# A fused adaLN transformer block: new places for transposes, reciprocals and statistics, and a small product moved to GpSimd

## The chip, the cores and the metric

The kernel runs on one core of a Trainium2 chip. A core has a matrix engine (TensorE, PE in the profile), a vector engine (VectorE, DVE), an activation engine (ScalarE, ACT), a general engine (GpSimd, POOL) and a queue engine (SyncE, SP) that here only issues DMAs. Each engine executes its own instructions in order and waits for others by semaphores. The metric is the time of one execution in microseconds on the device; lower is better. All arithmetic is in 32-bit floats.

## The reference

For 16 sequences (batches) of 1024 tokens with 256 features, an attention layer and a mixture-of-experts layer are computed, both behind a modulated layer norm:

```
mod = silu(c) @ wmod                              # shift, scale, gate, per batch, twice
h   = layernorm(x) * (1 + ca) + sa
xn  = layernorm(h) * gamma + beta
q, k = rope(xn Wq + bq), rope(xn Wk + bk);  v = xn Wv + bv     # 16 heads of 16
p   = softmax(causal(q k^T / 4));  o = (p v) Wo + bo
x   = x + ga * (h + o)
h2  = layernorm(x) * (1 + cb) + sb
x   = x + gb * scatter_add(experts(h2[top_idx]))  # 8 experts, 512 rows each, gelu
```

Two layer norms stand in front of attention, one on x and one on h. Each needs, per row, a mean, a variance, the power r = (variance + eps)^-0.5, and the product n = -mean * r; then the row is scaled by r and shifted by n.

## The kernel before

**The loop.** After a start (modulation, constants, batch 0's own preparation) the kernel runs one long loop: batch b, group G of four heads (0 to 3), step n (0 to 9). I write (G, n) for a place in it. A step treats one block of keys against the queries of one half of the sequence (c = 0: queries 0 to 511, c = 1: 512 to 1023); steps 1 and 5 treat two small blocks at once and are called two-block steps. In every step TensorE makes, for four heads, the scores `s` of this group (L682) and, one group ahead, the products `m` (L605) whose row maxima the next group will need. They come in two runs (bursts): scores of heads 0 and 1 with maxima products of heads 2 and 3, then the other way round. ScalarE takes the exponential of each `s` (L695), GpSimd zeroes what lies above the diagonal (L700), VectorE takes the maximum of each `m` (L623 and L627; the latter is a masked form with a separate accumulator read). `s` and `m` share six PSUM tiles.

**Between the runs and behind them.** TensorE does one item between the runs (`first`) and one behind the second (`second`). One is the product of the last step's probabilities with the values (`product(last)`, L729); the other is a piece for the next batches: the transposes `ptx` of the normalised rows (L485, evicted by ScalarE, L486), projections to queries and keys (L510, with two vector products each for the rotary angles, L517), to values (L541), or the output projection (L821). If there is no piece, the values are split into two halves. The transposes (`turns`) are placed in two-block steps: (0,1), (0,5), (1,1), (3,5). All these pieces share one other PSUM tile, `misc`.

**Normalising two batches ahead.** `steps_h` makes the norms. Its parts have names: `x0` to `x3` and `h0` to `h3` are statistics of a 256-wide row tile (VectorE, L387), `moments` merges them (L392), `power` makes r by two small GpSimd instructions (L397, L398), `less` makes n by one small vector instruction (L406), `norm` applies both (ScalarE, L415), and larger GpSimd passes scale, shift, add a bias, gate and add onto x. The table `H_AT` gives each part its place (G, n) for either half of the sequence. Parts of VectorE go into the list `inside`: they are taken one at a time behind each of the step's four maxima, and what is left is taken behind the last (`drain`). Parts of the other engines go into `extra`, which is emitted at the end of the step.

**The sums' inverse.** The values carry a column of ones, so each half's output ends with the softmax sums. When a half is done (c = 0 at step 3, c = 1 at step 0 of the next group), `finish` copies the output (ScalarE, L744), sends the sums to DRAM and back as `den` (two DMAs on SP, L784 and L785), and returns what is left: `inverse` (the reciprocal on VectorE, L789, a row to DRAM, L791, four broadcasts back as `rec`, L794), `scaled` (GpSimd, L797) and, in odd groups, `joined` (GpSimd, L800). `to_do` places them: the inverse into `inside` two steps after the half is done, the GpSimd parts at the end of the fifth step after it (c = 0) or the fourth (c = 1).

The orders on PE, VectorE, ScalarE and GpSimd are as written; SP's order comes from the scheduler and follows the program closely. After the loop come the experts, which the change does not touch.

Of the kernel before, what the change touches and what calls it, by code (L numbers as in the profile page):

```python
# [11 lines left out]
F32 = mybir.dt.float32  # L12
# [4 lines left out]
ALU = mybir.AluOpType  # L17
AX = mybir.AxisListType

P = 128  # L20
# [7 lines left out]
def adaln_block_kernel(  # L28
# [27 lines left out]
    nc = tc.nc  # L56
# [5 lines left out]
    NT = L // P  # L62
    GH = 4
# [5 lines left out]
    TC = QC // P  # L69
# [7 lines left out]
    eps = const.tile([P, NT], F32, name="eps")  # L77
    nc.vector.memset(eps, EPS)
    mhalf = const.tile([P, NT], F32, name="mhalf")
    nc.vector.memset(mhalf, -0.5)  # L80

    C, E = top_idx.shape
# [113 lines left out]
    with ExitStack() as actx:  # L196
# [178 lines left out]
        def steps_h(b, half, named=False):  # L375

            s = S[b]
            mine = {}  # L380
            passes = nc.vector if (b, half) == (0, 0) else nc.gpsimd

            def stat(of, i):
                if i == 0:
                    mine["st"] = wk.tile([P, TC, 6], F32, name=f"st_{of}_{b}_{half}", tag="st")
                src = s["x"][:, half * TC + i, :] if of == "x" else s["h", half][:, i, :]
                nc.vector.bn_stats(mine["st"][:, i, :], src)  # L387

            def moments(of):
                mine["mv"] = wk.tile([P, TC, 2], F32, name=f"mv_{of}_{b}_{half}", tag="mv")  # L390
                for i in range(TC):
                    nc.vector.bn_aggr(mine["mv"][:, i, :], mine["st"][:, i, :])  # L392
                mine["mean"] = mine["mv"][:, :, 0]

            def power(of):
                mine["r"] = wk.tile([P, TC], F32, name=f"rstd_{of}_{b}_{half}", tag="rstd")
                nc.gpsimd.tensor_tensor(mine["r"], mine["mv"][:, :, 1], eps[:, :TC], ALU.add)  # L397
                nc.gpsimd.tensor_tensor(mine["r"], mine["r"], mhalf[:, :TC], ALU.pow)  # L398

            def whole(of):  # L400
                moments(of)
                power(of)

            def less_mean(of):
                mine["n"] = wk.tile([P, TC], F32, name=f"nmr_{of}_{b}_{half}", tag="nmr")
                nc.vector.scalar_tensor_tensor(mine["n"], mine["mean"], -1.0, mine["r"], ALU.mult, ALU.mult)  # L406

            def norm(of, u):
                if of == "x" and u == 0:
                    s["h", half] = lk.tile([P, TC, D], F32, name=f"h_{b}_{half}", tag="h")  # L410
                if u == 0 and not named:
                    less_mean(of)
                h = s["h", half]
                for i in (2 * u, 2 * u + 1):
                    nc.scalar.activation(  # L415
                        h[:, i, :],
                        s["x"][:, half * TC + i, :] if of == "x" else h[:, i, :],
                        AF.Identity,
                        bias=mine["n"][:, i : i + 1],
                        scale=mine["r"][:, i : i + 1],  # L420
                    )

            def row(n):
                return (bo_bc[:, None, :] if n is None else s["mod"][:, n : n + 1, :]).to_broadcast([P, 2, D])

            def turn(u, n, op):
                h = s["h", half][:, ts(u, 2), :]
                passes.tensor_tensor(h, h, row(n), op)  # L428

            def rest(u, n, op):  # L430
                if n is None and u == 0 and b > 0:
                    mine["rest"] = lk.tile([P, TC, D], F32, name=f"r_{b}_{half}", tag="r", bufs=1)
                elif n is None and u == 0:
                    if half == 0:
                        s["rest"] = big_tile([P, NT, D], "r_0")
                    mine["rest"] = s["rest"][:, ts(half, TC), :]
                r = mine["rest"][:, ts(u, 2), :]
                (passes if n is None else nc.gpsimd).tensor_tensor(r, s["h", half][:, ts(u, 2), :] if n is None else r, row(n), op)

            def onto(u):  # L440
                xh = s["x"][:, half * TC + 2 * u : half * TC + 2 * u + 2, :]
                nc.gpsimd.tensor_tensor(xh, xh, mine["rest"][:, ts(u, 2), :], ALU.add)

            if named:
                pieces = {f"{of}{i}": lambda of=of, i=i: stat(of, i) for of in "xh" for i in range(TC)}
                for of in "xh":
                    pieces[of + " moments"] = lambda of=of: moments(of)
                    pieces[of + " power"] = lambda of=of: power(of)
                    pieces[of + " less"] = lambda of=of: less_mean(of)
                for u in range(2):  # L450
                    pieces[f"x norm{u}"] = lambda u=u: norm("x", u)
                    pieces[f"scale{u}"] = lambda u=u: turn(u, 1, ALU.mult)
                    pieces[f"shift{u}"] = lambda u=u: turn(u, 0, ALU.add)
                    pieces[f"bias{u}"] = lambda u=u: rest(u, None, ALU.add)
                    pieces[f"h norm{u}"] = lambda u=u: norm("h", u)
                    pieces[f"gate{u}"] = lambda u=u: rest(u, 2, ALU.mult)
                    pieces[f"onto{u}"] = lambda u=u: onto(u)
                return pieces

            return (  # L460
                [("v", lambda i=i: stat("x", i)) for i in range(TC)]
                + [("g", lambda: whole("x"))]
                + [("v", lambda u=u: norm("x", u)) for u in range(2)]
                + [("g", lambda u=u: turn(u, 1, ALU.mult)) for u in range(2)]
                + [("g", lambda u=u: turn(u, 0, ALU.add)) for u in range(2)]
                + [("v", lambda i=i: stat("h", i)) for i in range(TC)]
                + [("g", lambda: whole("h"))]
                + [("g", lambda u=u: rest(u, None, ALU.add)) for u in range(2)]
                + [("v", lambda u=u: norm("h", u)) for u in range(2)]
                + [("g", lambda u=u: rest(u, 2, ALU.mult)) for u in range(2)]  # L470
                + [("g", lambda u=u: onto(u)) for u in range(2)]
            )
# [410 lines left out]
        def steps(places):  # L883
# [7 lines left out]
        OUT = steps([(0, 9), (0, 9), (), ()]), steps([(), (), (0, 2, 8, 9), ()])  # L891

        H_AT = (
            "x0 0 3, x1 0 4, x2 0 6, x3 0 8, x moments 0 9, x power 1 0, x less 1 3, x norm0 1 3, x norm1 1 4, "
            "scale0 1 4, shift0 1 4, scale1 1 6, shift1 1 7, h0 1 8, h1 1 9, h2 2 0, h3 2 2, h moments 2 3, h power 2 3, "
            "bias0 2 4, h less 2 4, bias1 2 6, gate0 2 6, gate1 2 6, h norm0 2 7, onto0 2 7, h norm1 2 8, onto1 3 3",
            "x0 1 4, x1 1 6, x2 2 4, x3 2 6, x moments 2 8, x power 2 9, x less 3 2, x norm0 3 2, x norm1 3 4, "
            "scale0 3 3, shift0 3 4, scale1 3 6, shift1 3 6, h0 3 6, bias0 3 6, h1 3 7, h2 3 8, h3 3 8, bias1 3 8, "
            "gate0 3 9, h moments 3 9, h power 3 9, h less 4 3, h norm0 4 3, gate1 4 3, onto0 4 3, h norm1 4 4, onto1 4 3",
        )  # L900

        def place_h(b, half, at0):
            parts = steps_h(b, half, named=True)
            for entry in H_AT[half].split(", "):
                name, G, n = entry.rsplit(" ", 2)
                dve = name[:2] in ("x0", "x1", "x2", "x3", "h0", "h1", "h2", "h3") or name.endswith(("moments", "less"))
                (inside if dve else extra)[at0 + int(G) * NS + int(n)].append(parts.pop(name))
            assert not parts, parts.keys()

# [13 lines left out]
        with tc.manual_schedule(engines=ORDERED | {ET.SP}):  # L923
# [52 lines left out]
            units, place = maxima(0, 0)  # L976
# [78 lines left out]
        for e in range(E):  # L1055
            for t in range(NCT):
                extra[(B - 2) * NG * NS + e * NCT + t].append(
                    lambda e=e, t=t: gather(cw[:, e, t, :], combine[:, :], widx[:, t, e : e + 1])
                )
        def to_do(finish, c, step):  # L1060

            first, *others = finish(c)
            if step >= ((B - 1) * NG + NG - 1) * NS + mid:
                for n, item in enumerate([first, *others]):
                    extra[step + 1 + n].append(item)
                return
            inside[step + 2].append(first)
            extra[step + (4 if c else 5)].extend(others)

        behind = None  # L1070
        for b in range(B):
            for G in range(NG):
# [3 lines left out]
                for n, parts in enumerate(blocks):  # L1076
# [25 lines left out]
                    product = values if n else behind and behind[0]  # L1102
                    if not product:
                        first, second = [], mine
                    elif mine and units and len(last) == 2:
                        first, second = mine, [lambda: product(last)]
                    elif units and len(mine) == 2:
                        first, second = [lambda: product(last), mine[1]], mine[:1]
# [263 lines left out]
```

## Time and profile before

| what | us |
|---|---|
| median of three runs | 2889.95 |
| the runs | 2884.34, 2889.95, 2890.49 |
| the profiled execution | 2886.74 |
| its span, first to last instruction | 2885.0 |
| PE busy | 2810.8 |
| VectorE busy | 2125.2 |
| ScalarE busy | 1651.1 |
| GpSimd busy | 1562.6 |

The attention loop fills the span from about 95 to 2605 us, about 164 us a batch; the experts follow. TensorE is counted as busy nearly all of the loop, with a mean granted clock of 0.986 of full speed over the span. Its matmuls are pipelined and their ends are modelled, so a matmul that starts late because a PSUM tile isn't free can leave no idle time in the count: the starts in the timeline tell more. In the timeline a row is: start, duration, engine, line, operation, output and inputs, shapes, count; a bracket gives the idle time before it and what ended it.

### The profile page before, as it was taken

Reading aid. Unit: us, or ns where it says so; the run is one execution under the profiler, and the core shown is the slowest. Engines: PE = TensorE matmul, PEld = TensorE weight load, DVE = VectorE, ACT = ScalarE, POOL = GpSimd, SP = SyncE. Lnnn points to the kernel's source line nnn. Section 1 sums busy time; section 2 is a strip of 40 time slices with the busy share of each in tenths; the row PEclk is TensorE's granted clock in tenths of the full one; section 3 lists DMA queues with packets and bytes.
Section 4 is the critical chain, followed back from the end, with each engine's and each line's share of the span. In section 5 each row is a group of like instructions: output and inputs, shape, how many; then the busy total and the mean of one; then the engine's idle time right before and its main releaser. Section 6 shows DMA issues by size and latency. Waiting matters only on the chain.

```text
span 2885.0 us, 62886 instructions
## 1 busy us (share of the span) xinstructions
PE 2810.8 (97%) x22373; PEld 1289.4 (45%) x22373; DVE 2125.2 (74%) x6810; ACT 1651.1 (57%) x3342; POOL 1562.6 (54%) x2063
## 2 busy tenths in 40 slices
PE   5899999999999999999999999999999999997998
PEld 3444444444444444444444444444444444443665
DVE  5777878777787878787877878787878777763554
ACT  2356666666666566666666666656666655653111
POOL 5455464546555555546454655555464666354553
PEclk7899999999999999999999999999999999998999
DMA  4211121222222222212222222222121212134552
GB/s 122 58 44 35 50 71 52 64 56 68 59 56 56 64 61 63 60 51 66 63 59 62 64 54 58 60 67 62 50 71 51 75 41 65 32 95 153 176 184 67
DMA packets 200154, 199.58 MB, mean 69 GB/s; under 512 B 93344, under 2 KB 154208, under 8 KB 199840
## 3 DMA queue, kind: packets, MB, share of 16 engines
q1 hardware_dynamic: 172240, 147.69, 18.9%
q0 software_dynamic: 8448, 24.78, 2.7%
q10 hardware_dynamic: 19152, 23.08, 2.6%
q8 instruction: 177, 2.90, 0.4%
q14 instruction: 137, 1.12, 0.1%
HBM read 118.67 MB, written 75.66 MB: 67 GB/s over the span
## 4 chain that ended last, share of the span: by engine, by line
PE 90%; DMA 3%; DVE 2%; POOL 2%; issue 1%; ACT 1%; SPq 0%; POOLq 0%; DVEq 0%; ACTq 0%
PE s L682 39%; PE o L729 20%; PE pqk L510 9%; PE m L605 7%; PE pw L821 4%; PE pv L541 4%; PE fo L1229 2%; PE ph L1204 2%; PE ptx L485 1%; DMA out_dram<-fy,idx 1%; DMA cur<-out_dram,idx 1%; POOL modg L98 1%; ACT p L695 0%; DMA ops<-rot 0%; DVE nmr_h L406 0%
## 5 line engine op out<-in xcount | busy, mean ns | idle before, releaser
L695 ACT ACTIVATE p<-s 128x512 f32<-128x512 f32 (+1 forms) x2560 | 1278.9, 552 | 895.5 <-PE m L605 797.4
L605 PE MATMUL m<-ko,qo 32*128 32x512 f32 (+3 forms) x6144 | 1439.5, 527 | 7.0 <-DVE mt L623 4.7
L682 PE MATMUL s<-qo,ko 32*128 32x512 f32 (+3 forms) x6144 | 1359.1, 526 | 0.6 <-DMA qo<-max 0.5
L700 POOL TENSOR_SCALAR_AFFINE_SELECT p<-p 128x256 f32<-128x256 f32 x1024 | 416.1, 414 | 1002.4 <-ACT p L695 1001.2
L623 DVE TENSOR_REDUCE mt<-m 128x1 f32<-128x512 f32 x1024 | 673.0, 683 | 203.9 <-PE m L605 184.2
L682 PEld LDWEIGHTS s<-qo,ko 32*128 32x128 f32 x6144 | 514.8, 183 | 597.3 <-issue 423.6
L729 PE MATMUL o<-p,v_pad 128*32 128x512 f32 (+3 forms) x6840 | 652.7, 464 | 3.2 <-POOL p L700 2.8
L627 DVE CUSTOM_DVE_ANT_0 masked<-m,dmask,mt 128x256 f32<-128x256 f32 (+3 forms) x1024 | 511.4, 539 | 142.6 <-PE m L605 132.1
L627 DVE CUSTOM_DVE_ANT_0 masked<-m,dmask 128x512 f32<-128x512 f32 (+3 forms) x1024 | 453.9, 485 | 189.3 <-PE m L605 170.2
L605 PEld LDWEIGHTS m<-ko,qo 32*128 32x128 f32 x6144 | 576.6, 184 | 30.2 <-DVE mt L627 11.2
L729 PEld LDWEIGHTS o<-p,v_pad 128*32 128x32 f32 x6840 | 149.0, 108 | 427.8 <-issue 180.0
L510 PE MATMUL pqk<-xnT,wqk 128*128 128x256 f32 x1024 | 287.3, 405 | 1.8 <-ACT xnT L486 1.3
L510 PEld LDWEIGHTS pqk<-xnT,wqk 128*128 128x128 f32 x1024 | 175.3, 190 | 193.0 <-issue 148.5
L428 POOL TENSOR_TENSOR h<-h,mod 128x512 f32<-128x512 f32 x124 | 157.6, 1274 | 76.5 <-ACT h L415 70.9
L627 DVE DVE_READ_ACCUMULATOR2_ANT mt<- 128x1 f32 x2048 | 168.7, 82 | 0.0
L541 PE MATMUL pv<-wv_sb,xnT 128*128 128x256 f32 x512 | 146.9, 410 | 1.1 <-ACT xnT L486 0.9
L821 PE MATMUL pw<-wo,onT 128*128 128x256 f32 x512 | 144.2, 405 | 0.6 <-DVE onT L778 0.6
L1207 ACT ACTIVATE gT<-ph,b_sb 128x512 f32<-128x512 f32 x64 | 44.0, 687 | 174.1 <-PE ph L1204 169.1
L541 PEld LDWEIGHTS pv<-wv_sb,xnT 128*128 128x128 f32 x512 | 87.9, 191 | 98.5 <-issue 76.5
L517 DVE SCALAR_TENSOR_TENSOR rot<-pqk,bcol,cosT 128x256 f32<-128x256 f32 x256 | 122.0, 477 | 11.6 <-PE pqk L510 8.3
L821 PEld LDWEIGHTS pw<-wo,onT 128*128 128x128 f32 x512 | 86.9, 189 | 89.3 <-issue 70.9
L517 DVE SCALAR_TENSOR_TENSOR rot<-pqk,bcol,sinT 128x256 f32<-128x256 f32 x256 | 121.3, 474 | 0.6 <-DMA ops<-rot 0.6
(122 smaller groups left out, 2239.5 us busy)
## 6 DMA issues: line engine op xcount, KB each, us to landing
ops<-rot SPq DMA_DIRECT2D x128, 256.0 KB
rec<-rec_d SPq DMA_DIRECT2D x504, 32.0 KB
rows<-y SPq DMA_DIRECT2D x62, 256.0 KB
out_dram<-y SPq DMA_DIRECT2D x62, 256.0 KB
w<-in_W_dram SPq DMA_DIRECT2D x14, 1024.0 KB
qo<-ops SPq DMA_DIRECT2D x192, 64.0 KB
ko<-ops SPq DMA_DIRECT2D x192, 64.0 KB
x<-in_x_dram ACTq DMA_DIRECT2D x24, 512.0 KB
```

Source lines behind the costliest of these rows:

```text
L428: passes.tensor_tensor(h, h, row(n), op)
L510: nc.tensor.matmul(ps, lhsT=wqk[:, k, n, e, :], rhs=xt[:, k, ts(u, QW)], start=(k == 0), stop=(k == KC - 1))
L517: nc.vector.scalar_tensor_tensor(s["rot", half, n, e, f][:, ts(u, QW)], ps, bcol[:, n, e : e + 1], tab[:, half * QC + u * QW : half * QC + ...
L541: nc.tensor.matmul(pv, lhsT=S[b]["xnT", t // TC][:, k, ts(t % TC, P)], rhs=wv_sb[:, k, :], start=(k == 0), stop=(k == KC - 1),)
L605: nc.tensor.matmul(sc[:, sum(w[:n]) : sum(w[: n + 1])], lhsT=q[rows, ts(i, P)], rhs=k[rows, c * QC : c * QC + w[n]], start=True, stop=True,)
L623: nc.vector.tensor_reduce(dst, sc[:, 0:w], AX.X, ALU.max, negate=True)
L627: nc.vector.tensor_tensor_reduce(out=masked[:, 0:w], in0=sc[:, 0:w], in1=dmask[:, QC - w : QC], scale=-1.0, scalar=mt[half][:, 0, h, i % T ...
L682: nc.tensor.matmul(sc[:, o:e], lhsT=k[rows, ts(j_, P)], rhs=q[rows, c_ * QC + q0 : (c_ + 1) * QC], start=True, stop=True,)
L695: nc.scalar.activation(p[:, h, 0:end], sc[:, 0:end], AF.Exp, scale=scale)
L700: nc.gpsimd.affine_select(out=mine, in_=mine, compare_op=ALU.is_ge, fill=0.0, base=0, pattern=[[0, 3 - n], [0, n], [1, P]], channel_multip ...
L729: nc.tensor.matmul(acc[c][W * g : W * (g + 1), q0:q1], lhsT=v[:, j, h * VW + 1 - DH * (G % 2) : h * VW + 1 - DH * (G % 2) + W], rhs=p[:, g ...
L821: nc.tensor.matmul(po, lhsT=s["onT", c][:, k, ts(t, P)], rhs=s["wo"][:, k, :], start=(k == 0), stop=(k == KC - 1),)
```

## The change

It has four parts. (1) In a two-block step that has a piece (a turn), the piece goes between the two runs and the values behind the second; before, the values went between and the piece behind. (2) `power` now also makes n, by two GpSimd multiplications (mean times r, times a constant tile of -1), and the vector instruction `less` is gone, with its places in `H_AT`. (3) The inverse of c = 0 moves from step + 2 to step + 3, with three empty items in front of it, so that it is taken behind the step's last maximum; `scaled` and `joined` stay where they were. (4) In `H_AT`, `x2` of the first half moves from (0,6) to (0,8) and `x3` from (0,8) to (0,9); of the second half `x0` moves from (1,4) to (1,0), `x1` from (1,6) to (1,4), and `x3` from (2,6) to (2,8).

The order of instructions changes accordingly: 64 vector instructions fewer (and one more constant), 128 GpSimd instructions more, no difference in TensorE's work. On SP's queue, the row and broadcasts of c = 0's inverse come behind two stores of rotated rows in group 1, and, in the last batch's group 2, behind the load of an expert's weights.

```diff
@@ constants
+    minus = const.tile([P, NT], F32, name="minus")
+    nc.vector.memset(minus, -1.0)
@@ power(of)
                 nc.gpsimd.tensor_tensor(mine["r"], mine["r"], mhalf[:, :TC], ALU.pow)
+                mine["n"] = wk.tile([P, TC], F32, name=f"nmr_{of}_{b}_{half}", tag="nmr")
+                nc.gpsimd.tensor_tensor(mine["n"], mine["mean"], mine["r"], ALU.mult)
+                nc.gpsimd.tensor_tensor(mine["n"], mine["n"], minus[:, :TC], ALU.mult)
...
-            def less_mean(of):
-                mine["n"] = wk.tile([P, TC], F32, name=f"nmr_{of}_{b}_{half}", tag="nmr")
-                nc.vector.scalar_tensor_tensor(mine["n"], mine["mean"], -1.0, mine["r"], ALU.mult, ALU.mult)
...
@@ H_AT (first half)
-            "x0 0 3, x1 0 4, x2 0 6, x3 0 8, x moments 0 9, x power 1 0, x less 1 3, x norm0 1 3, x norm1 1 4, "
+            "x0 0 3, x1 0 4, x2 0 8, x3 0 9, x moments 0 9, x power 1 0, x norm0 1 3, x norm1 1 4, "
...
@@ H_AT (second half)
-            "x0 1 4, x1 1 6, x2 2 4, x3 2 6, x moments 2 8, x power 2 9, x less 3 2, x norm0 3 2, x norm1 3 4, "
+            "x0 1 0, x1 1 4, x2 2 4, x3 2 8, x moments 2 8, x power 2 9, x norm0 3 2, x norm1 3 4, "
...
@@ to_do
+        def nothing():
+            pass
...
-            inside[step + 2].append(first)
+            inside[step + (2 if c else 3)].extend([first] if c else [nothing] * (GH - 1) + [first])
             extra[step + (4 if c else 5)].extend(others)
@@ the loop
-                    elif mine and units and len(last) == 2:
+                    elif mine and units and 2 in (len(last), len(parts)):
                         first, second = mine, [lambda: product(last)]
```

## The prediction

> **What bounds the kernel now.** I read the page's engine shares and chain first, then the timeline of the attention loop piece by piece, then the views of the changed lines.
>
> ```profile
> PE 2810.8 (97%) x22373; PEld 1289.4 (45%) x22373; DVE 2125.2 (74%) x6810; ACT 1651.1 (57%) x3342; POOL 1562.6 (54%) x2063
> PEclk7899999999999999999999999999999999998999
> PE 90%; DMA 3%; DVE 2%; POOL 2%; issue 1%; ACT 1%; SPq 0%; POOLq 0%; DVEq 0%; ACTq 0%
> ```
>
> TensorE is the bound, and the change takes no matmul away. But a busy PE here isn't a PE at its peak, so I took from the timeline the time from each matmul group's first start to the next group's. It repeats to 2 ns: 1.07 us for a burst 512 wide, 0.858 for 384, 0.886 in a two-block step, 1.06 for a projection, 0.586 for the four transposes, 0.57 to 1.00 for values. What lies above these is waiting: 104 us over the loop, about 4.5 us in a median batch of 164 us. Only that can be won. (G, n) is group G, step n.
>
> **1, the turns** (four two-block steps a batch: (0,1), (0,5), (1,1), (3,5)). Now the transposes stand behind the second run, and the next step's fourth tile waits for the first maximum of that run:
>
> ```profile
> 1223.45 0.66 PE L485 MATMUL ptx<-ident,h 128*128 128x128 f32 x4
> 1224.03 0.58 PE L682 MATMUL s<-qo,ko 32*128 32x384 f32 x1
> 1224.13 0.08 DVE L627 DVE_READ_ACCUMULATOR2_ANT mt<- 128x1 f32 x1
> 1224.27 0.58 PE L605 MATMUL m<-ko,qo 32*128 32x384 f32 x1
> ```
>
> Three tiles start by 1224.06, the fourth at 1224.27, right after the accumulator read: six PSUM tiles, and this one is needed back. The waits are 0.22, 0.34, 0.22 and 0.28 us, 1.06 a batch. Afterwards the transposes lie between the runs, and the second run starts 0.886 + 0.586 = 1.47 us behind the first, as the next step does now behind the second. Its fourth tile needs the first run's first maximum, done about 1.7 us after the run's start (now: run at 1222.56, tile at 1224.27). So the same 0.2 to 0.35 us should appear one run earlier. The split values at (2,1) and (3,1), with 0.57 us between the runs, wait 0.217 there. In (0,5) the transposes moreover meet a PSUM tile whose sine product ends at 1237.21, 0.25 us after they could start; that overlaps the same wait. Bounds over 15 batches: -16 us if nothing reappears, +2 if the longer masked maximum adds 0.03 a step. I take +1, by the split rows.
>
> **2, means times powers by GpSimd.** 64 vector instructions go, 128 GpSimd ones come.
>
> ```profile
> L406 DVE SCALAR_TENSOR_TENSOR nmr_x<-mv_x,rstd_x x32: 149/156/349, 23.0 to 2288.3; 128x4 f32<-128x4 f32 x32
> L406 DVE SCALAR_TENSOR_TENSOR nmr_h<-mv_h,rstd_h x32: 150/600/3710, 38.8 to 2331.6; 128x4 f32<-128x4 f32 x32
> ```
>
> The same 4 columns take 0.15 or over 1 us, and 3.71 once. Each long one runs over large GpSimd passes, ending with one:
>
> ```profile
> 1311.70 1.30 POOL L797 TENSOR_TENSOR part<-oT,rec 128x512 f32<-128x512 f32 x1
> 1311.97 1.05 DVE L406 SCALAR_TENSOR_TENSOR nmr_h<-mv_h,rstd_h 128x4 f32<-128x4 f32 x1
> 1312.94 0.68 DVE L623 TENSOR_REDUCE mt<-m 128x1 f32<-128x512 f32 x1
> ...
> 2331.54 1.27 POOL L438 TENSOR_TENSOR r<-r,mod 128x512 f32<-128x512 f32 x1
> 2331.56 3.71 DVE L406 SCALAR_TENSOR_TENSOR nmr_h<-mv_h,rstd_h 128x4 f32<-128x4 f32 x1
> 2332.76 2.48 POOL L442 TENSOR_TENSOR x<-x,r 128x512 f32<-128x512 f32 x2
> 2335.93 1.01 PE L605 MATMUL m<-ko,qo 32*128 32x512 f32 x1 [1.00 <-DVE mt L623]
> ```
>
> The first stands at (2,4): the maxima behind it run 1 us late, and (2,5) waits 0.29 + 0.60 us. In batch 10, where the instruction took 0.15, (2,5) waits 0.37. The difference, about 0.52, occurs in 12 batches: -6.2 us; batch 0 -0.5. The second stands in batch 14: two steps take 14.0 us against 8.25, -5.7; the granted clock is 0.50 from 2336.2 to 2343.0. In the start two long ones (1.2 us) lie on the chain; two GpSimd multiplies of the size of the addition at L397 (0.20) replace each: about -1.2 for both.
> The cost: 64 x 0.41 = 26 us more on GpSimd. It is hidden by gaps before the selects (GpSimd sat idle 1002 us waiting for the exponentials); at (3,9), the tightest, the select moves from 1376.8 to 1377.2 and its values start at 1379.1. Without cover it would be 0.41 a place, +26.
> [...]
>
> **3, the inverse of the first half's sums.** 63 reciprocals (0.25 us) move from behind (G,5)'s first maximum to behind (G,6)'s last, about 6 to 7 us later. Now they wait for den's DMA only in G = 2: 0.26 to 1.2 us in five batches, with 0.34 to 1.28 us of PE wait at (2,6), 4.3 us together. That goes: -4.3. Behind it is queued the next step's first maximum, which needs a matmul that ends later anyway. Late next is rec: row to DRAM (1.42 us from issue to the next issue), four broadcasts (1.3 us of issues, then about 2.0 us to landing), 4.7 us. With the inverse at 1283.8 in (1,6) of batch 7, rec lands by 1289; GpSimd reaches the product at 1289.16. In G = 0, 2, 3 I get 1.4, 2.8 and 0.2 us to spare. On SP's queue, in G = 1, two rotary stores now go first; they issue by 1282.4 and wait for GpSimd passes that end at 1281.8, so the row isn't held. A product 1 us late delays selects that have about 2 us: 0. In the last batch a 1 MB weight load goes ahead too; there too the product comes some 4 us later: 0, at worst +3.
>
> **4, three statistics elsewhere.** 0.42 us each. Those leaving (1,6) and (2,6) free the maximum that (1,7) and (2,7) wait for: 0.24 there against 0.07 at (0,7) and (3,7). -0.17 in 11 to 13 batches each: -3.8 (0 at worst, if the inverse takes the room). The arrivals at (1,0), (0,9) and (2,8) find VectorE with about 0.2 us to spare or more before the next maximum is needed: 0, at worst 0.1 a place, +4.
>
> **5, what the removal does to the second half's inverse.** At (3,2) the queue between the maxima was nmr_x, then the inverse; now the inverse comes one maximum earlier, and it waits for den:
>
> ```profile
> 1500.36 0.16 DVE L406 SCALAR_TENSOR_TENSOR nmr_x<-mv_x,rstd_x 128x4 f32<-128x4 f32 x1
> 1500.44 0.55 DVE L627 CUSTOM_DVE_ANT_0 masked<-m,dmask 128x384 f32<-128x384 f32 x1
> 1502.49 0.25 DVE L789 RECIPROCAL inv<-den 128x16 f32<-128x16 f32 x1 [1.50 <-DMA den<-den_d]
> 1502.66 0.49 DVE L627 CUSTOM_DVE_ANT_0 masked<-m,dmask 128x384 f32<-128x384 f32 x1
> 1503.22 1.12 PE L605 MATMUL m<-ko,qo 32*128 32x512 f32 x2
> ```
>
> The DMA sets 1502.49. The maximum at 1500.44 now comes after it, 0.49 us more work before the tile that PE waits for. In 12 of batches 0 to 13 the present wait (0.86 to 2.46 us) already reaches PE: +0.49 each, +0.3 for the other two, +6.2 (0 if den comes sooner, +8 by 0.58 a batch, which batch 14's order, without nmr_x, suggests).
>
> **Sum.** +1 - 6.2 - 0.5 - 5.7 - 1.2 - 4.3 - 3.8 + 6.2 = -14.5 us. The profiled execution took 2886.74 (span 2885.0 and 1.74 around it): 2872.2. The median of the three runs lies 3.2 above it: 2875.4, so I say 2875.
>
> **Rivals.**
> - The turns' wait really goes: the second run's fourth tile could profit from idle VectorE time. Against it stand the split rows. -16 instead of +1: 2858.
> - The waits don't leave: tiles, maxima and PE form a ring of six buffers, so a removed wait may return at the next step. For it: (0,6) waits 0.34 and (0,7) then only 0.07, (1,6) waits nothing and (1,7) 0.24. And the 3.71 us accident may not be in every run (the shots spread 6 us, its size). If parts 3, 4 and the accident give nothing: 2889, no change.
> - The other side: the earlier inverse at (3,2) holds VectorE longer than 0.49, because PE gets there sooner while den hangs on SP's queue (den's issue stands behind the maxima's round trip and operand loads). Each 0.1 us costs 1.3 us in 13 batches; from 1.1 us more the whole gain is gone. Gaps of 1.6 us then stand in PE, like the 1.58 before 2335.9 that the half clock followed, at 3.4 us each. With 1 us more and four such drops: 2875 + 13 + 14 = 2902.
> [...]
>
> **How the numbers follow.** My forecast has 0.50; the turns' gain 0.12; no change 0.22; the hold at (3,2) 0.16. Some 0.2% (6 us) is what a measurement can tell from no change. Faster: 0.50 + 0.12 + a quarter of no change, 0.67; same 0.17; slower 0.16. The range reaches to the rivals: 2860 at the low end (just above the first), 2892 at the high end, which leaves out most of the hold. The forecast's own range is 2866 to 2884.
>
> **What would show it.** After: no long small product on VectorE, small GpSimd ones of 0.2 us; (2,5) waiting 0.37; (1,7) and (2,7) 0.07; the second run of turn steps stretched by 0.2 to 0.35; no wait for den at first-half inverses; at (3,2) the inverse behind the first maximum, with den waits of 1 to 3 us and (3,3) later by 0.5; GpSimd reaching rec without idling over 1 us. I am wrong if turn steps lose their waits altogether, if GpSimd idles for rec by several us, or if the (3,3) wait grows by over 1 us.

## The result and the profile after

| | us |
|---|---|
| before, median of four runs | 2887.14 (2884.28 to 2890.49) |
| after, median of four runs | 2868.98 (2868.05 to 2870.84) |
| ratio, 95% interval | 0.9933 (0.9917 to 0.9950) |
| profiled execution after (span) | 2869.37 (2867.7) |

The change gained 18 us. The predicted 2875 lay 6 us too high, with the result inside the forecast's own range of 2866 to 2884. The page of the changed kernel, engine shares, granted clock by slices and chain:

```profile
PE 2791.3 (97%) x22373; PEld 1275.1 (44%) x22373; DVE 2112.1 (74%) x6747; ACT 1650.1 (58%) x3342; POOL 1587.6 (55%) x2191
...
PEclk8899999999999999999999999999999999998999
...
PE 93%; DVE 2%; POOL 1%; DMA 1%; issue 1%; ACT 1%; POOLq 0%; SPq 0%; DVEq 0%; ACTq 0%
```

TensorE is still the bound, and still looks 97% busy. GpSimd has 25 us more work, as priced. That says little, so I took from both timelines the start of every step and compared step by step. This is the mean change per batch over batches 1 to 13, in us; every step not listed changed by under 0.03:

```
part 1, turns        (0,1) +0.20  (0,2) -0.22   (0,5) +0.36  (0,6) -0.34
                     (1,1) +0.21  (1,2) -0.22   (3,5) +0.41  (3,6) -0.28   sum +0.12
part 2, product      (2,5) -0.48
part 3, inverse      (2,6) -0.27
part 4, statistics   (1,7) -0.17  (2,7) -0.12
part 5, side effect  (3,2) +0.04  (3,3) +0.15
span: start -0.85, batch 0 -1.78, batches 1 to 13 -9.97, batch 14 -6.11, last batch and experts +1.34 = -17.4
```

(Batches 1 to 13 take 156 to 158 us each in both kernels, batch 0 171 to 173; the 164 told ahead was a misreading, which no term of the sum used.)

The turn at (0,1) in batch 7 of the changed kernel, from the timeline (start, duration, engine, line, operation, tiles):

```profile
1213.36 0.66 PE L483 MATMUL ptx<-ident,h 128*128 128x128 f32 x4
...
1213.94 0.48 PE L680 MATMUL s<-qo,ko 32*128 32x256 f32 x1
...
1213.95 0.48 PE L603 MATMUL m<-ko,qo 32*128 32x256 f32 x1
1214.03 0.48 PE L680 MATMUL s<-qo,ko 32*128 32x256 f32 x1
...
1214.04 0.08 DVE L625 DVE_READ_ACCUMULATOR2_ANT mt<- 128x1 f32 x1
...
1214.18 0.48 PE L603 MATMUL m<-ko,qo 32*128 32x256 f32 x1
...
1216.02 0.58 PE L680 MATMUL s<-qo,ko 32*128 32x384 f32 x1
...
1216.03 0.58 PE L603 MATMUL m<-ko,qo 32*128 32x384 f32 x1
...
1216.03 0.58 PE L680 MATMUL s<-qo,ko 32*128 32x384 f32 x1
...
1216.04 0.58 PE L603 MATMUL m<-ko,qo 32*128 32x384 f32 x1
```

The transposes now stand in front of the step's second run. Of that run three tiles start by 1214.03 and the fourth at 1214.18, behind the accumulator read at 1214.04. The next step's four tiles start together. The same wait has moved one run forward.

The small product's groups and the GpSimd passes that wait for the broadcasts (count, busy time, mean ns, then idle time ahead of them and what ended it):

```profile
L795 POOL TENSOR_TENSOR part<-oT,rec 128x512 f32<-128x512 f32 x62 | 78.9, 1272 | 29.7 <-DMA rec<-rec_d 28.7 <-issue 0.8
...
L402 POOL TENSOR_TENSOR nmr_h<-mv_h,rstd_h 128x4 f32<-128x4 f32 x32 | 6.5, 203 | 2.5
L403 POOL TENSOR_TENSOR nmr_h<-nmr_h,minus 128x4 f32<-128x4 f32 x32 | 6.5, 203 | 2.5
```

The product is on GpSimd at 0.203 us an instruction, as estimated. GpSimd waits 28.7 us for `rec` in front of these products of the odd groups (8.1 before), up to 2.6 us at a time and once, in the last batch, 4.5 us. That is more than I had worked out, but no step of batches 1 to 13 that follows starts later.

And the place at (3,2), in batch 12, where the wait for `den` is long:

```profile
2119.12 1.09 PE L680 MATMUL s<-qo,ko 32*128 32x512 f32 x2 [0.45 <-DMA qo<-max]
...
2119.39 0.25 DVE L787 RECIPROCAL inv<-den 128x16 f32<-128x16 f32 x1 [2.81 <-DMA den<-den_d]
2119.56 0.51 DVE L625 CUSTOM_DVE_ANT_0 masked<-m,dmask 128x384 f32<-128x384 f32 x1
...
2119.99 0.08 DVE L625 DVE_READ_ACCUMULATOR2_ANT mt<- 128x1 f32 x1
2119.99 0.55 DVE L625 CUSTOM_DVE_ANT_0 masked<-m,dmask 128x384 f32<-128x384 f32 x1
...
2120.13 0.69 PE L603 MATMUL m<-ko,qo 32*128 32x512 f32 x1
...
2120.61 0.69 PE L603 MATMUL m<-ko,qo 32*128 32x512 f32 x2
```

VectorE stands 2.81 us for the sums. Three masked maxima are queued behind the inverse, and the `m` tiles of (3,3) start only as these finish: 2120.13, 2120.61. The two steps (3,2) and (3,3) together take 7.64 us when nothing waits; here they take 9.55.

### The profile page after: what moved, and what is told of

It is laid out like the page before. It is cut to its first block, busy times and chain, and to the rows that moved or that the text cites. A ratio compares the mean times of both kernels' runs of the same rounds, so it can differ in the third digit from the quotient of the medians.

```text
span 2867.7 us, 62991 instructions
## 1 busy us (share of the span) xinstructions
PE 2791.3 (97%) x22373; PEld 1275.1 (44%) x22373; DVE 2112.1 (74%) x6747; ACT 1650.1 (58%) x3342; POOL 1587.6 (55%) x2191
## 4 chain that ended last, share of the span: by engine, by line
PE 93%; DVE 2%; POOL 1%; DMA 1%; issue 1%; ACT 1%; POOLq 0%; SPq 0%; DVEq 0%; ACTq 0%
PE s L680 40%; PE o L727 20%; PE pqk L508 8%; PE m L603 5%; PE pv L539 5%; PE pw L819 5%; PE fo L1231 4%; PE ph L1206 4%; PE ptx L483 1%; DVE mt L621 1%; DVE rot L515 1%; DMA max<-mr 0%; DMA ops<-rot 0%; PE fpt L1195 0%; ACT p L693 0%
## 5 line engine op out<-in xcount | busy, mean ns | idle before, releaser
L603 PE MATMUL m<-ko,qo 32*128 32x512 f32 (+3 forms) x6144 | 1414.3, 527 | 3.9 <-DVE mt L621 3.6
L680 PEld LDWEIGHTS s<-qo,ko 32*128 32x128 f32 x6144 | 522.1, 183 | 598.5 <-issue 365.5
L603 PEld LDWEIGHTS m<-ko,qo 32*128 32x128 f32 x6144 | 559.0, 184 | 19.2 <-DVE mt L621 8.0
```

The costliest lines, as they stand in the source:

```text
L603: nc.tensor.matmul(sc[:, sum(w[:n]) : sum(w[: n + 1])], lhsT=q[rows, ts(i, P)], rhs=k[rows, c * QC : c * QC + w[n]], start=True, stop=True,)
L680: nc.tensor.matmul(sc[:, o:e], lhsT=k[rows, ts(j_, P)], rhs=q[rows, c_ * QC + q0 : (c_ + 1) * QC], start=True, stop=True,)
```

## The experiments

Each kernel was timed in five rounds beside the kernel before on the same chip. "Before" is that chip's median; the bracket is the 95% interval of the ratio.

| kernel | us | before | ratio |
|---|---|---|---|
| turns_only | 2892.18 | 2886.97 | 1.0017 [1.0008, 1.0026] |
| power_only | 2878.05 | 2886.97 | 0.9969 [0.9957, 0.9981] |
| inverse_stats_only | 2877.15 | 2886.97 | 0.9968 [0.9957, 0.9979] |
| all_but_turns | 2869.40 | 2886.97 | 0.9938 [0.9924, 0.9951] |
| late_second_half | 2854.75 | 2885.03 | 0.9893 [0.9878, 0.9909] |
| late_no_turns | 2853.51 | 2885.03 | 0.9891 [0.9876, 0.9906] |
| columns | 2873.43 | 2885.03 | 0.9959 [0.9945, 0.9973] |
| turns_stats | 2884.00 | 2885.03 | 0.9996 [0.9987, 1.0005] |
| inverse_only | 2883.12 | 2888.83 | 0.9985 [0.9976, 0.9994] |
| power_twice | 2869.73 | 2888.83 | 0.9929 [0.9915, 0.9942] |
| late_columns | 2858.67 | 2888.83 | 0.9894 [0.9879, 0.9909] |
| one_tensor | 2859.20 | 2885.60 | 0.9911 [0.9895, 0.9928] |

### One part at a time

**turns_only**: the kernel before with part 1.

```diff
-                    elif mine and units and len(last) == 2:
+                    elif mine and units and 2 in (len(last), len(parts)):
```

> The kernel before with the turns between the two runs of the two-block steps and nothing else. My theory (the wait for the first maximum moves one run earlier and keeps its size): 0.22 us less behind (0,1) and (1,1) and 0.20 more inside them, about +0.02 at (0,5) and +0.1 at (3,5), in sum 0 to +2 us. Rival (the turns are what gains, the second run profits from idle VectorE time): the inner waits stay under 0.1 us and the time falls by 8 us or more.

Measured: 5.2 us slower, a miss. The four turn steps shift exactly as in the changed kernel. Two things come on top: +0.17 a batch at (0,7) and +0.14 at (2,6). At (0,6) stood the statistic `x2`; the old order's wait at (0,6) had hidden it. At (2,6) the first half's inverse waits for `den`; that wait is also 0.14 longer in power_only and 0.13 in columns, which leave the turns alone, so it isn't shown to come from the turns.

**all_but_turns**: the changed kernel without that line.

> The changed kernel with the turns put back behind the second run. My theory: the turns are worth about +0.08 us a batch, so this is 1 us faster than the changed kernel, 18 to 20 below before. Rival (the turns carry part of the gain once the inverse has left the two-block steps): 4 us or more slower than the changed kernel.

Measured: 2869.40, the same as with turns (2868.98). Beside the other parts the turns are worth nothing that can be told from nothing.

**turns_stats**: parts 1 and 4 together on the kernel before.

> The kernel before with the change of turns and the three statistics moved, and nothing else. Turns alone cost 5 us. My theory: of these, 0.17 us a batch (2.5 us) come from the statistic that still stood at (0,6), where the old order of turns hid it, and show as a wait at (0,7); with the statistic moved to (0,8) that goes, and the statistics' own gain, 0.17 at (1,7) and 0.12 at (2,7), comes on top: 2887 + 5.2 - 2.5 - 4.2 = 2885.5, with (0,7) at its old 0.07. The rival: the turns cost 5 us of themselves and the statistics give their 4: the wait at (0,7) stays, or another of the same size takes its place, 2888.

Measured: 1.0 us under before, with no change left at (0,7). So the 0.17 at (0,7) (2.5 us over 15 batches) was the statistic at (0,6), and part 4 takes it away. The +0.16 at (2,6) stayed; part 3 takes that wait away altogether. The turns' loss in isolation is thus mostly waits that parts 3 and 4 remove: 2.5 us at (0,7) and about 2 at (2,6).

**power_only**: part 2 alone.

```diff
+                mine["n"] = wk.tile([P, TC], F32, name=f"nmr_{of}_{b}_{half}", tag="nmr")
+                nc.gpsimd.tensor_tensor(mine["n"], mine["mean"], mine["r"], ALU.mult)
+                nc.gpsimd.tensor_tensor(mine["n"], mine["n"], minus[:, :TC], ALU.mult)
...
-                nc.vector.scalar_tensor_tensor(mine["n"], mine["mean"], -1.0, mine["r"], ALU.mult, ALU.mult)
```

> The kernel before with the product of means and powers by GpSimd and nothing else (the inverse of the second half at (3,2) thereby comes one maximum earlier). My theory: (2,5) falls from 0.29 + 0.60 us of wait to 0.37 (-6.5 us over the loop), the stall of several us where a small product takes 3.7 us can't happen (-5.7 where the run before had it), the start gains about 1, and (3,3) loses 0.3 to 0.5 a batch (+4 to +6): 6 to 9 us below the median of before. Rival (a removed wait returns at the next step of the ring of six PSUM tiles): within 2 us of before.

Measured: 8.9 us faster. (2,5) -0.48 a batch, the stretch in batch 14 gone (-5.5 in that batch), the start -1.2, (2,6) +0.14, (3,3) +0.28.

**inverse_stats_only** and **inverse_only**: parts 3 and 4, and part 3 alone.

```diff
-            inside[step + 2].append(first)
+            inside[step + (2 if c else 3)].extend([first] if c else [nothing] * (GH - 1) + [first])
```

> The kernel before with the first half's inverse behind (G,6)'s last maximum and the three statistics moved, nothing else. My theory: no wait for den at the first halves (-4.3 us), (1,7) and (2,7) wait 0.07 in place of 0.24 (-4): 8 us below before, with (2,5) and (3,3) as before. Rival (ring): within 2 us of before, the waits turning up at (G,8) or (G,9). Second rival (rec comes late): GpSimd's products wait several us and values behind them too: above before.

> The kernel before with the first half's inverse moved behind the last maximum of the step after, and nothing else. My theory: this takes the wait at (2,6), 0.27 us a batch, and leaves 0.24 and 0.2 at (1,7) and (2,7), which belong to the statistics: 0.27 x 15 = 4, so 4 to 5 us under the kernel before, and about 4 to 5 above the version with inverse and statistics together. The rival: the inverse, which stood at (1,6) and (2,6) too, shares in the waits at (1,7) and (2,7); then these fall already here and this is as fast as both together, 9 to 10 us under the kernel before.

Measured: 9.8 and 5.7 us faster by the medians (for the inverse alone 4.3 by the ratio, 1.7 to 6.9 by its interval). With the inverse alone no inverse of a first half waits for `den` any more, (2,6) falls by 0.27 a batch, and (1,7) and (2,7) don't fall (0.00 and +0.05). With the statistics they fall by 0.17 and 0.12. Each wait had one owner, as told. In both the 3.71 us product of batch 14 is still there.

Alone the three give +5.2 - 8.9 - 9.8 = -13.5, together -18: the difference is about what the turns lose when alone.

### Is the work moved to GpSimd really covered?

**power_twice**: in the changed kernel GpSimd multiplies by -1 three times, which leaves n the same.

```diff
-                nc.gpsimd.tensor_tensor(mine["n"], mine["n"], minus[:, :TC], ALU.mult)
+                for _ in range(3):
+                    nc.gpsimd.tensor_tensor(mine["n"], mine["n"], minus[:, :TC], ALU.mult)
```

> The changed kernel with GpSimd multiplying by minus one three times instead of once, for all means: 128 more instructions of 0.20 us, 26 us of GpSimd's time, in the places where the change has put as much. My theory: the gaps before the selects hide it, as they hid the first 26 us: 2869, give or take 1.5, with at most 0.8 us of it in the start (two places on its chain, 0.41 each). The rival: the cover was just used up; then up to 0.41 us a place show at the steps whose selects come next, up to 20 us more, 2875 to 2889.

Measured: 2869.73, ratio 0.9929 against 0.9933. Another 26 us of GpSimd's time cost nothing, so the first 26 were covered with room to spare.

### What is left at (3,3)

**late_second_half**: in the changed kernel also the second half's inverse of group 2 stands behind the last maximum of (3,2).

```diff
-            inside[step + (2 if c else 3)].extend([first] if c else [nothing] * (GH - 1) + [first])
+            G = (step // NS - 1) % NG if c else None
+            late_ = [nothing] * (GH - 1) if not c or G == 2 else []
+            inside[step + (2 if c else 3)].extend(late_ + [first])
```

> The changed kernel, with one thing more: of group 2, the inverse of the second half's sums at (3,2) stands behind that step's last maximum instead of its first. My theory: the wait that is left at (3,3), 0.64 us a batch in the changed kernel, is VectorE standing for the denominators' transfer (30.3 us over the batches) in front of the masked maxima, so it falls to under 0.1 us: -0.55 to -0.6 in 14 or 15 batches, -8 to -9 us, and no half clock behind it; about 2860.5 us. The rival: the inverse is only wanted early because GpSimd needs the reciprocal rows; it comes about 2.5 us later, GpSimd reaches its product later, the selects at (3,9) or (0,0) come late, and the wait moves there: 2869, give or take 2.

Measured: 2854.75, 14 us under the changed kernel by the medians, 11.5 by the two ratios (the chips' medians before differ by 2.1), 14.7 by the profiles. The timeline of batch 12 at the same place:

```profile
2109.51 0.55 DVE L625 CUSTOM_DVE_ANT_0 masked<-m,dmask 128x384 f32<-128x384 f32 x1
...
2109.68 0.69 PE L680 MATMUL s<-qo,ko 32*128 32x512 f32 x1
...
2109.69 0.69 PE L603 MATMUL m<-ko,qo 32*128 32x512 f32 x1
...
2109.70 0.69 PE L680 MATMUL s<-qo,ko 32*128 32x512 f32 x1
...
2109.70 0.69 PE L603 MATMUL m<-ko,qo 32*128 32x512 f32 x1
...
2109.99 0.25 DVE L787 RECIPROCAL inv<-den 128x16 f32<-128x16 f32 x1
```

The maxima no longer stand behind the transfer, and the inverse finds `den` there. The four tiles of (3,3) start within 0.02 us. Summed over batches 0 to 14, the steps (3,2) and (3,3) take more than their 7.64 us a batch by this much (called the excess below):

```
before 9.1 us    changed 12.7    late_second_half 0.8    (one_tensor, below: 4.8)
```

That is 12.0 us of the gain. Of these, 3.2 are in batch 0, which the expectation of 8 to 9 had not counted apart and where the changed kernel loses clock. The stretches of 4 us around it (times, busy us of PE, PEld, DVE, ACT and POOL, granted clock, DMA share, GB/s), first the changed kernel:

```profile
237.00:241.00 4.00, 3.21 (x20) 1.08 (x16) 2.74 (x9) 2.31 (x5) 3.79 (x4) 0.91 0.14 31
241.00:245.00 4.00, 4.00 (x24) 1.40 (x20) 1.33 (x3) 1.75 (x4) 2.87 (x3) 0.67 0.14 27
```

and the late inverse:

```profile
236.00:240.00 4.00, 3.52 (x44) 1.36 (x40) 2.58 (x7) 3.28 (x7) 2.94 (x4) 1.00 0.12 23
240.00:244.00 4.00, 4.00 (x32) 1.46 (x28) 2.60 (x5) 2.68 (x6) 3.70 (x3) 1.00 0.12 35
```

**late_no_turns**: the same without the change of turns.

> The same late inverse of group 2's second half, without the change of turns. As the turns were worth nothing beside the rest (2869.4 without them against 2869.0 with them), the theory gives the same time as with them, within 2 us, and the wait at (3,3) gone as there: 2859 to 2863 us. If the maxima at (3,5) or (0,1) only keep up because of the turns once the inverse is out of the way, it lies 3 us or more above the version with turns.

Measured: 2853.51, the fastest of all kernels run, 1.2 us under the version with turns on the same chip, less than the two scatter. The turns are not needed.

### Why was the small product long?

**columns**: the kernel before, with the product still on VectorE at its old places, in four instructions of one column.

```diff
-                nc.vector.scalar_tensor_tensor(mine["n"], mine["mean"], -1.0, mine["r"], ALU.mult, ALU.mult)
+                for i in range(TC):
+                    nc.vector.tensor_scalar(
+                        mine["n"][:, i : i + 1], mine["mean"][:, i : i + 1], mine["r"][:, i : i + 1], -1.0, ALU.mult, ALU.mult
+                    )
```

> The kernel before, with the mean times the power still on VectorE at its old places, but as four instructions of one column each, which take the power as their scalar operand, so that each reads one tensor in place of two. My theory: the instruction is long (1.05 and 3.71 us) because it reads two tensors and so shares its way into memory with GpSimd's passes; four with one tensor each take about 4 x 0.08 to 0.15 us, over GpSimd passes too, none over 0.35, the wait at (2,5) falls from 0.85 to about 0.4 or 0.5 and the step of 3.71 us in batch 14 is gone: 2887 - 6 - 5.7, and up to +3 for the longer queue, so 2875 to 2878. The rival: anything that VectorE does in that place while GpSimd passes run is held, or the instruction waits for data: some of the four are as long as before, 2887 or, with four to be held, above it.

Measured: 2873.43, 11.6 us under before. None of 256 instructions took over 0.215 us (count, then shortest, median and longest ns):

```profile
L407 DVE TENSOR_SCALAR nmr_x<-mv_x,rstd_x x128: 191/204/215, 22.8 to 2278.2; 128x1 f32<-128x1 f32 x128
L407 DVE TENSOR_SCALAR nmr_h<-mv_h,rstd_h x128: 203/204/215, 38.7 to 2321.5; 128x1 f32<-128x1 f32 x128
```

Batch 14's place in the timeline, where the kernel before held VectorE for 3.71 us over these passes:

```profile
2321.14 1.28 POOL L441 TENSOR_TENSOR r<-r,mod 128x512 f32<-128x512 f32 x1
2321.16 0.57 DVE L407 TENSOR_SCALAR nmr_h<-mv_h,rstd_h 128x1 f32<-128x1 f32 x4
...
2321.65 2.05 DVE L626 TENSOR_REDUCE mt<-m 128x1 f32<-128x512 f32 x3
...
2322.36 2.50 POOL L445 TENSOR_TENSOR x<-x,r 128x512 f32<-128x512 f32 x2
```

The first column starts 0.02 us into the pass, just as the long product did, and nothing is held.

**one_tensor**: the changed kernel, with an extra instruction of four columns that reads one tensor at the old places in the loop. Its result is not used.

```diff
+                less = wk.tile([P, TC], F32, name=f"less_{of}_{b}_{half}", tag="less")
+                nc.vector.tensor_scalar(less, mine["mean"], -1.0, None, ALU.mult)
...
```

> The changed kernel, where at each of the old places of the small product in the loop VectorE again executes an instruction of the same four columns, but one that reads a single tensor (the means times minus one, into a tile that nobody reads); GpSimd goes on making the means times powers. My theory: the second tensor makes the long ones, so none of these is over 0.25 us, (2,5) stays within 0.05 us of its 0.37, and there is no step of 3.71 us in batch 14. At (3,2) the inverse stands behind the second maximum again, as before the change; if the 3.6 us that (3,2) to (3,4) took more in the changed kernel come from that place, they go: 2869 - 3.6 + 0.5, 2865 to 2867, else 2869 to 2870. The rival: any instruction of four columns (or any that reads the means) in that place is held by GpSimd's passes: about 1 us at (2,4) and 3.7 in batch 14 again, 2878 to 2881.

Measured: 2859.20, under the changed kernel by 9.8 us by the medians, 6.4 by the two ratios and 11.6 by the profiles; and the theory of the second tensor falls. The group, then two places of the timeline:

```profile
L407 DVE TENSOR_SCALAR less_h<-mv_h x28: 157/362/3734, 203.0 to 2309.5; 128x4 f32<-128x4 f32 x28
```

```profile
1295.44 1.28 POOL L441 TENSOR_TENSOR r<-h,bo_bc 128x512 f32<-128x512 f32 x1
...
1296.38 0.36 DVE L407 TENSOR_SCALAR less_h<-mv_h 128x4 f32<-128x4 f32 x1
...
1296.68 1.30 POOL L800 TENSOR_TENSOR part<-oT,rec 128x512 f32<-128x512 f32 x1
...
2309.45 1.27 POOL L441 TENSOR_TENSOR r<-r,mod 128x512 f32<-128x512 f32 x1
2309.47 3.73 DVE L407 TENSOR_SCALAR less_h<-mv_h 128x4 f32<-128x4 f32 x1
...
2310.68 2.49 POOL L445 TENSOR_TENSOR x<-x,r 128x512 f32<-128x512 f32 x2
...
2313.85 0.69 PE L608 MATMUL m<-ko,qo 32*128 32x512 f32 x1 [1.01 <-DVE mt L626]
```

An instruction with one tensor is held too. At (2,4) it starts late in a pass and ends at 1296.74 with it (1296.72). In batch 14 it starts 0.02 us into the first of three passes that follow each other and ends at 2313.20, behind the third (2313.17). So what the runs show is: an instruction of four columns in SBUF, with one tensor or two, that starts inside a GpSimd pass of 1.3 us ends when a pass ends (in the kernel before, all 18 that took over 0.3 us end 0.01 to 0.03 us behind a GpSimd instruction); one that starts just ahead of a pass takes 0.15 (at 1783.71 in the kernel before, 0.06 ahead of one); four of a single column, with the power as scalar operand, are not held (0.19 to 0.22 us in all 256). Whether the size of one or the scalar operand saves them was not separated. By what means a pass holds the instruction, no run shows; the shared way into memory was a conjecture of mine. Why the instruction of batch 14 was held through three passes (3.71 and 3.73 us), while elsewhere (1296.74) one got in between two, stays open.

The gain of this run comes in the main from another place. With the extra instruction back at (3,2), the inverse stands behind the second maximum again: the excess there is 4.8 us instead of 12.7. I had expected 3.6 less and got 7.9; so the side effect of the removal (part 5) is real, and the extra instruction more than pays for itself. Batch 14's step cost 2.7 us of it. Of the rest of the 11.6 us, 2.9 lie ahead of the first step of the loop and 2.8 in the last batch and the experts; nothing here explains them.

**late_columns**: late_no_turns with the product by columns on VectorE.

> The version with both inverses late and no change of turns, with the means times powers made by VectorE in four instructions of one column each (0.20 us each) in place of two by GpSimd. My theory: at (3,2) 0.82 us now stand between the first and the second masked maximum, where the late inverse has left no wait behind which they could hide; the maxima there come every 0.86 us and take 0.55 to 0.65, so 0.3 to 0.6 us a batch show at (3,3), and 0.03 at (2,5): 5 to 9 us above the version with GpSimd, 2858 to 2863. The rival: the six tiles give enough room, and the start gains as it did with the columns alone: the same as with GpSimd, 2852 to 2855.

Measured: ratio 0.9894 against 0.9891 with GpSimd, on two chips whose medians before differ by 3.8 us; the two profiles differ by 5.0 us. The wait that my theory named isn't there: (3,2) and (3,3) together gain 0.06 a batch where 0.3 to 0.6 were expected, so that theory falls. Whether columns or GpSimd is better is not settled; GpSimd isn't slower.

## Why the prediction was right, and where it was off

**Turns, +1.** Right: the wait reappears one run earlier (+0.12 a batch by the steps, 1.8 us over 15 batches; by the medians the kernel without the turns was 0.4 us slower, too little to tell). In (3,5) it became 0.47 us, more than the 0.35 told. What the prediction didn't see was that the old wait at (0,6) covered a statistic; it cost nothing only because part 4 moves that statistic.

**The product by GpSimd, -13.6 with its cover.** Right in size: -0.48 x 13 = -6.2 at (2,5) against -6.2, -5.7 at (0,4) of batch 14 against -5.7, the start -0.85 against -1.2 (not more than starts differ between profiles). The cover held, shown by doubling the cost. The bare durations in the traces are 0.15 us on VectorE against 0.41 for the two instructions on GpSimd; they decide nothing here.

**The first half's inverse, -4.3.** Right: (2,6) -0.27 x 15 = -4.1; the kernel with that alone gained 4.3 (1.7 to 6.9). The working by which `rec` lands just before GpSimd reaches the product was too favourable (28.7 us of idle), yet its cover held: no PE cost in the steps. Idling for `rec` "by several us" was one of the prediction's own signs of being wrong. It did occur, 4.5 us once and up to 2.6 otherwise, so what failed there is the sign, which asked for more than PE needs.

**The statistics, -3.8.** Right: (0.17 + 0.12) x 15 = -4.4.

**The second half's inverse, +6.2: right in total, wrong in its parts.** In this pair of profiles the excess at (3,2) and (3,3) rose from 9.1 to 12.7, +3.6. One pair says little here, because `den` lands earlier or later with the rest: in single batches the excess goes both ways (batch 8: 0.65 to 0.00; batch 5: 0.47 to 1.40). The other kept profiles tell more. This is the excess over batches 0 to 14, first with the old product on VectorE, then with GpSimd's:

```
before 9.1   turns_only 8.2   inverse_only 7.9   inverse_stats_only 7.4   turns_stats 7.5     mean 8.0
changed 12.7   all_but_turns 13.7   power_only 14.4   power_twice 15.9                        mean 14.2
```

The two groups don't overlap, and their means differ by 6.2. (columns with 6.7 and one_tensor with 4.8, which keep another instruction of VectorE at the place, lie on the side of the first.) But the working is not what the runs show. The step that was off is "In 12 of batches 0 to 13 the present wait (0.86 to 2.46 us) already reaches PE: +0.49 each": in the kernel before, only 9 of these 14 batches lie more than 0.05 us above 7.64. Between the groups' means, batches 1 to 14 rise by 4.1 us, 0.29 each, and batch 0 alone by 2.1; in the changed kernel the clock drops to half there for 3.41 us (from 240.25). The prediction counted such a drop with its rival only. That the total fits is thus in part luck. A wait for a transfer isn't a constant onto which queued work can be added.

**The sum.** It gave -14.5, and the profiles differ by 17.4. Of that difference, 2.6 us are what this pair shows less at (3,2) and (3,3) than the term. Another 3.2 us fell at (0,4), (0,8) and (2,3) of batch 0, which no term names; the 1.2 us at (0,4) go in every kernel with GpSimd's product and in none of the others, so they came with it, while the rest follows no single part. The other way go 1.3 us behind batch 14 and 1.2 at (1,4) of that batch, which no term names either. So the sum came as close as it did partly because these cancel. The other 3 us of the 6 by which 2875 was too high are the 3.2 that were added because the median of the three runs lay above the profiled execution: with the fourth run that median is 2887.14, 0.4 above it. The medians differ by 18.2.

**The rivals.** The turns' wait didn't go; removed waits didn't return at the next step (all other steps changed by under 0.03 us); the hold at (3,2) was the right place, but far from the 1 us a batch that this rival needs. Its drop of the clock did come, once, in batch 0 (3.41 us at half, from 240.25).

What I missed is that the largest sum to be had lay in the term I counted as a cost: moving that one inverse too gives another 11.5 us (by the ratios) to 14 (by the medians).

## What to carry to other kernels

A wait for a transfer in an in-order queue costs whatever stands behind it (2.81 us of waiting for `den` at (3,2) of batch 12, with 9.55 us for two steps that take 7.64): put the waiting instruction behind the work that another engine needs next, and look at each removed instruction for what it had kept behind itself. A tiny VectorE instruction on SBUF can be held by GpSimd passes for many times its own length (up to 3.73 us for one of 0.15); cut it so that it isn't held (0.19 to 0.22 us a column here), or give it to GpSimd where that has idle time. An edit that loses alone can be free beside others that remove what it exposes, so measure parts alone and left out.

## What the runs showed of the hardware that I had not expected

- An instruction of 0.15 us on VectorE took up to 3.73 us under GpSimd passes of 1.3 us, with one tensor as input too; statistics of 256 columns from SBUF took their 0.42 us over such passes (in the kernel before, 0.37 to 0.43 for all 256).
- The granted clock drops on a grid. In the traces of the kernel before and of the changed kernel every stretch of half clock, but for the one that the end of the trace cuts off, lasts one to five times 3.413 us; the shortest is 3.41 (from 240.25 in the changed kernel), the longest 17.07 (from 2633.1 in the kernel before). In the kernel before the drops at 2336.2 and 2633.1 are 87.0 times 3.413 us apart, in the changed kernel those at 240.3 and 2612.5 are 695.0 times. The same gap of 1.0 us behind the held instruction of batch 14 was followed by half clock in the kernel before (TensorE 0.71 busy in the 3.41 us ahead of the drop at 2336.2), and not in one_tensor (granted clock 1.00 from 2312 to 2316; matmuls of 512 columns at 2316.49 take 0.69 us, against 1.22 at 2340.39 in the half clock of the kernel before). This may account for some of the scatter of the kernel before, by my estimate; only one of its executions was profiled. Busy share alone doesn't decide it: the stretch of 3.4 us that ends at 2578.5 in the kernel before was 0.54 busy and no drop followed.
